# Layer 0's scores: bias and mask added per head on VectorE in the eviction, instead of in one GpSimd addition, with a newly searched order

## The chip, the cores and the metric

The kernel runs on one core of a Trainium2 chip. A core has TensorE (PE, matrix products, results into PSUM), VectorE (DVE), ScalarE (ACT), GpSimd (POOL) and SyncE (SP, which here issues all DMAs). Each engine works through its own queue in order; semaphores order the engines among each other. The metric is the device time of one execution in microseconds (us). The kernel before takes 2370.53 us, the median of three runs (2370.43 to 2375.34).

## The reference, cut to what matters

Two decoder layers work on 64 sequences of 64 tokens with 256 features. Layer 0 is self attention (16 query heads, 4 key/value heads of 128, layer norm and rotary embedding on queries and keys), cross attention with a context, and a feed-forward part with a routed low-rank term; layer 1 is again self attention, cross attention and a feed-forward part. The change concerns the scores of layer 0's self attention:

```python
q = _layernorm(q, qn_g, qn_b)
k = _layernorm(k, kn_g, kn_b)
q = q * cos + _rotate_half(q) * sin
k = k * cos + _rotate_half(k) * sin
...
scores = jnp.einsum('bhqd,bhkd->bhqk', q, k) / jnp.sqrt(jnp.float32(D))
causal = jnp.triu(jnp.ones((s, s), dtype=bool), k=1)
scores = jnp.where(causal, -jnp.inf, scores)
weights = jax.nn.softmax(scores, axis=-1)
attn = jnp.einsum('bhqk,bhkd->bhqd', weights, v)
```

## The kernel before, in words

The 4096 tokens are worked in 16 groups of 256 tokens (four sequences). Phase "a" takes every group through layer 0 (`l0_attn`, `l0_xattn`, `l0_ffn`), phase "b" through layer 1 (`l1_attn`, `l1_xattn`, `l1_ffn`); between the two the group's activations are parked in DRAM. Weight preparation ("setup") runs beside the first groups.

`l0_attn` (L841) works a group in two blocks `blk` of eight query heads and two key heads, 32 blocks in all. In a block, keys, values and four pairs of query heads are projected (`proj2`, `proj_tok`, the three products of split fp16 numbers at L430 to L432) and rotated (`rope_bank`: ACT L832 and L833, DVE L834, POOL L835 and L837). The layer norm of the queries is not applied to the queries: its scale `rs` (a reciprocal root, the DVE chain L606 to L614 that ends in `nr_y`) is applied to the scores, and the query's bias gives a term of its own. So a row of scores is

    s1 = rs * (rotated q . k) + (rotated bias of q . k) + mask

The steps of it, in program order:

- DVE L908 and POOL L911 make the final keys `kf`.
- PE L919 multiplies the rotated bias with the keys into `bias_ps`, DVE L922 adds the causal mask and makes `bm`: 128 partitions (two sequences of 64 queries) x 4 x 64, one row of 64 for each half `j` of the group and each of the two key heads. Four query heads share one row.
- For each half `j`, PE L933 multiplies queries and keys for eight heads into `s_ps`, one bank of PSUM, 128 x 8 x 64, and DVE L935 takes it out with one `tensor_tensor` that multiplies by `rs`, into half of `s1` (128 x 16 x 64, fp32, in SBUF).
- POOL L937 adds `bm` to the whole of `s1` in one instruction of 1024 columns. POOL does not touch PSUM anywhere in this kernel.
- `e.gate` (L939 before, see L1004 and L1009) is the last of these instructions; the DMAs that load the next context tiles of `l0_xattn` are made to follow it.
- `softmax_rows` (L618): DVE L625 row maximum, POOL L626 subtraction, ACT L628 exponential, the sum (DVE L643, or POOL L640 and DVE L641), DVE L644 and POOL L645 the reciprocal, POOL L652 the scaling, ACT L654 and POOL L655 the split into two fp16 halves `phl`. Then a transposing DMA (L578) makes `pt` and PE L689 multiplies it with the values (`pv_block`), and `o_proj` (L709) adds the result to the residual `xt`.

In the same phase the cross attention's row maxima run on DVE (L1040, 512 instructions), its exponentials on ACT (L1074), its products on PE (L1033, L1067, L1083).

The order of all work is fixed before the kernel is built. Every step is declared with `s.o` (engine, cost in ns, what it reads and writes, the function that issues it) or `s.alt` (a choice of engines); `Sched.plan` (L255) is a list scheduler that walks through a planned time, at each step takes among the steps that can start first the one with the smallest due time, and emits the instructions in the order of their planned starts. The due times come from `PACE`, `SHIFT`, and two tables of offsets, `LEAD` (by tile name) and `FINE` (by step); `EPS`, `PEN`, `HOLD`, `SPACE`, `WINDOW` are further settings of the scheduler. `HOLD` is added to the due time of a PE step that would change the tiling of the array; `SWITCH` is what the plan charges for such a change. The tables were found by a search. Tiles come from pools by class: `B` is the eight banks of PSUM, `k4` holds `s1`, `k2` 67 tiles of 2 KiB a partition.

Of the kernel before, what the change touches and what calls it, by code (L numbers as in the profile page):

```python
# [20 lines left out]
S = 64  # L21
# [15 lines left out]
HOLD = 965  # L37
# [372 lines left out]
def c_dve(n, ap=0):  # L410
    return 72 + 1.042 * n + 63 * ap
# [429 lines left out]
def l0_attn(e, xt):  # L841
# [5 lines left out]
    for blk in range(2):  # L847
# [77 lines left out]
        for j in range(2):  # L925
            sps = s.T("B", [128, 8, S], name="s_ps")

            def f(*r, j=j):
                q, k, p = r[:4], r[4], r[5]
                for h in range(8):  # L930
                    for b in range(2):
                        t = slice(128 * j + 64 * b, 128 * j + 64 * b + 64)
                        nc.tensor.matmul(p[64 * b:64 * b + 64, h, :], q[h // 2][:, h % 2, t], k[:, h // 4, t], start=True, stop=True)  # L933
            s.o("PE", 1080, qu + [kf], [sps, s1.sub(j)], f, duty=0.65, tile=3)
            s.o("DVE", c_dve(512), [sps, rs], [s1.sub(j)], lambda p, r, t, j=j: nc.vector.tensor_tensor(  # L935
                t[:, 8 * j:8 * j + 8, :], p, bc(r[:, j, 0:2, :].rearrange("p a b -> p (a b)"), 2, S), ALU.mult))
        s.o("POOL", 2303, [bm], [s1], lambda b, t: nc.gpsimd.tensor_tensor(  # L937
            t.rearrange("p (a h) s -> p a h s", h=4), t.rearrange("p (a h) s -> p a h s", h=4), bc(b, 2, 4), ALU.add))
# [906 lines left out]
def ctx_scale(e, I, nt):  # L1845
# [15 lines left out]
EPS = 41.35  # L1861
PEN = 247.38
NQ = 1
LEAD = {
    ".xt": -7500, "a0.acc": 6500, "a0.bias_ps": -16000, "a0.bm": -112500, "a0.k_ps": -6000, "a0.kf": -4000,
    "a0.ku": -27000, "a0.ln_mv": 86500, "a0.ln_nb": -120000, "a0.ln_rs": 43000, "a0.ln_st": 60500, "a0.nr_v": -2500,
    "a0.nr_y": -92000, "a0.ohl": -35000, "a0.phl": -9500, "a0.po": -500, "a0.pt": 36500, "a0.qu": -2500,
    "a0.rb": 21500, "a0.rk": 2000, "a0.s1": -4500, "a0.s_ps": -27500, "a0.sm_mx": 120000, "a0.sm_sm": -2500,
    "a0.sq": -2000, "a0.ss": 15500, "a0.ss_t": -7000, "a0.sss": 30500, "a0.sw": 38000, "a0.v_ps": -50000,
    "a0.vt": 84000, "a0.vx": 111500, "a0.xT": -26500, "a0.xh": 112500, "a0.xhl": -29000, "a0.xt": -3000,  # L1870
    "a1.ctx1": -38500, "a1.k1": -120000, "a1.k1_ps": -24500, "a1.ksh": 26000, "a1.kst": -32000, "a1.ln_mv": 96000,
    "a1.ln_nb": -55000, "a1.ln_rs": 68500, "a1.ln_st": 120000, "a1.o1_ps": 47500, "a1.oT1": 23000, "a1.pT": -31000,
    "a1.phl": -101000, "a1.q1": 119500, "a1.q1_d": -9500, "a1.q1_ps": -56500, "a1.q1hl": 26500, "a1.q1st": 120000,
    "a1.s1": 120000, "a1.s1_ps": -90500, "a1.sm_f": -3000, "a1.sm_mx": -76000, "a1.sm_sm": 104000, "a1.v1": 90000,
    "a1.vbd": 10500, "a1.xT": 37000, "a1.xh": -8500, "a1.xhl": -6000, "a1.xt": 73500, "f0.-": -112500,
    "f0.f0_ps": -19500, "f0.f0o_ps": -14500, "f0.hT": -69000, "f0.hm": -120000, "f0.hm_ps": 20500, "f0.ln_mv": -4000,
    "f0.ln_nb": 39000, "f0.ln_rs": 42000, "f0.ln_st": 52000, "f0.xT": 78000, "f0.xh": 24000, "f0.xhl": -18000,
    "f0.xt": -11000, "f1.f1ah": 114500, "f1.f1am": -13000, "f1.f1ix": -115500, "f1.f1o": -116500, "f1.f1o_ps": -4500,
    "f1.f1s2": 73500, "f1.f1sx": 81500, "f1.gu": 8500, "f1.gu_ps": -112500, "f1.hq": -53500, "f1.hqT": 93500,
    "f1.ln_mv": 81500, "f1.ln_nb": -116500, "f1.ln_rs": -3000, "f1.ln_st": 31000, "f1.sig": 32000, "f1.xh": -10500,  # L1880
    "f1.xq": -119500, "f1.xqT": 111000, "f1.xt": 30500, "setup.-": 15500, "setup.a1am": 100500, "setup.am_ps": -4000,
    "setup.bo_ps": 70500, "setup.bo_w": -46500, "setup.cen": -72500, "setup.ctx_a": 64000, "setup.ctxa1": 99000,
    "setup.f_t": -94500, "setup.f_w": 23000, "setup.fam": -23500, "setup.fw_ps": 40000, "setup.g_G": -68500,
    "setup.g_ps": -75500, "setup.g_w": -21000, "setup.l0cols": 87500, "setup.l0ek": 7500, "setup.l0eq": -32500,
    "setup.l0w0": -3500, "setup.l0w1": -120000, "setup.l0w2": 67000, "setup.l0w3": 14000, "setup.l0w4": 96000,
    "setup.n_am1": 11500, "setup.n_o": -60000, "setup.n_ps": -116500, "setup.n_v": 120000, "setup.n_w": -28500,
    "setup.nf": 31500, "setup.p2_ar": -85500, "setup.p2_p2": -64500, "setup.rope_t": -34000, "setup.rp_tmp": -49000,
    "setup.sqj": -80000, "setup.w_a1": -25000, "setup.w_a1o": -110500, "setup.w_am1": -59000, "setup.w_f0": -77500,
    "setup.w_hl": -18500, "setup.w_l0kv": 7000, "setup.w_l0o0": -4000, "setup.w_l0o1": -7500, "setup.w_l0q0": -77000,
    "setup.w_l0q1": 26000, "setup.w_n": 47000, "setup.w_x1ki0": -30500, "setup.w_x1ki1": -15500,  # L1890
    "setup.w_x1q0": -64500, "setup.w_x1q1": 14500, "setup.x1wki0": 18500, "setup.x1wki1": 116500,
    "setup.x1wn0": 33500, "setup.x1wn1": 41000, "setup.x1wn2": 77500, "setup.x1wn3": 56000, "setup.x1wq0": 25500,
    "setup.x1wq1": -93500, "setup.xtwo": -62500, "x0.-": -120000, "x0.cT": -11500, "x0.ctx": 9000, "x0.hl": -82000,
    "x0.hl_d": -42500, "x0.ln_mv": -10000, "x0.ln_nb": -71000, "x0.ln_rs": -118000, "x0.ln_st": -103000,
    "x0.mneg": -99500, "x0.mx_ps": -37500, "x0.so": -80000, "x0.xh": 24500, "x0.xmx": -105500, "x0.xo_ps": 3500,
    "x0.xot_ps": 49500, "x0.xpt": 13500, "x0.xrc": -17500, "x0.xs_ps": -16500, "x0.xt": -41000, "x0.xt_ps": 2500,
    "x0.y": -35000, "x0.yo": -82500, "x1.acc": -38000, "x1.cTs": -120000, "x1.chl": 68500, "x1.ctx": -50000,
    "x1.gac": 42000, "x1.gjk": -34000, "x1.gy_ps": 48000, "x1.k8": -29500, "x1.ln_mv": 74500, "x1.ln_nb": -119500,
    "x1.ln_rs": -55000, "x1.ln_st": 87000, "x1.ms": -111500, "x1.phl": 6000, "x1.pt": 64000, "x1.q8": -90000,
    "x1.qk_ps": 17500, "x1.rkL": 103000, "x1.rkb": -88500, "x1.rkb_ps": -49000, "x1.rms": 24500, "x1.s1": 120000,  # L1900
    "x1.s_ps": -120000, "x1.sm_mx": -22000, "x1.sm_sm": -68500, "x1.vn": 117000, "x1.vn_ps": 68000,
    "x1.x1esc": -45000, "x1.xT": 88000, "x1.xh": 116000, "x1.xhl": 117000, "x1.xt": 23500,
}
RESV = 1e+15
TMIN = {"setup.w_a1": 1457, "setup.w_l0kv": -4579, "setup.w_x1q1": 1916, "setup.x1wki1": -18878, "setup.x1wn0": 1785, "setup.x1wn2": -1297, "setup.x1wn3": -2931, "setup.x1wq1": -2255}
FINE = dict(a=[
    (0, 1, -19000), (1, 1, -500), (2, 1, -9000), (3, 1, -13000), (4, 1, 42000), (5, 1, 22500), (6, 1, -11000),
    (7, 1, 10000), (8, 1, 15500), (9, 1, -39000), (10, 1, 1500), (11, 1, -9500), (12, 1, -12500), (13, 1, -15500),
    (14, 1, -5000), (15, 1, 13000), (16, 1, 4000), (17, 1, 9000), (18, 1, -30500), (19, 1, 21500), (20, 1, -45000),
    (21, 3, 500), (24, 1, -34000), (25, 1, 14000), (26, 1, 30500), (27, 1, 5000), (28, 1, 5500), (29, 1, -9000),  # L1910
    (30, 1, 12500), (31, 1, 7500), (32, 1, 21500), (33, 1, 23500), (34, 1, -2000), (35, 1, 44500), (36, 1, -5000),
    (37, 1, 9000), (38, 1, 10500), (39, 1, 6500), (40, 1, 24000), (41, 1, 10000), (42, 1, 6500), (43, 1, 49000),
    (44, 1, -7000), (45, 1, 9500), (46, 1, 10000), (47, 1, 3000), (48, 1, 15500), (49, 1, 10000), (50, 1, 17000),
    (51, 1, -9500), (52, 1, 9000), (53, 1, 10000), (54, 1, 10500), (55, 1, 35500), (56, 1, 3500), (57, 1, 21000),
    (58, 1, 2500), (59, 1, 4000), (60, 1, -500), (61, 1, 1500), (62, 1, -44500), (63, 1, 2000), (64, 1, 21500),
    (65, 1, -37000), (66, 1, -49500), (67, 1, -14000), (68, 1, -5500), (69, 1, -7500), (70, 1, 1000),
    (71, 1, -12500), (72, 1, 38000), (73, 1, -1000), (74, 1, 500), (75, 1, -5000), (76, 1, 4500), (77, 1, 1000),
    (78, 1, 9000), (79, 1, 2500), (80, 1, -4500), (81, 1, 5000), (82, 1, -17000), (83, 1, -12500), (84, 1, 41500),
# [100 lines left out]
FOLD = [False, True]  # L2019
SPACE = (7285, 2674)  # L2020
BURST = 1
SHIFT = -31810.49
START = (0, 3e3, 15e3, 22e3, 40e3, 3e3, 30e3, 36e3, 60e3, 70e3)
PACE = dict(a=(81129.88, 2.24), b=(66158.31, 2.05))
STEP = (15e3, 60e3, 3e3, 5e3)
# [162 lines left out]
```

## Time and profile before

| what | value |
|---|---|
| median of three runs | 2370.53 us |
| the profiled execution | 2375.9 us, its span from first to last instruction 2374.1 us |
| phase a: last `xt` of `o_proj` (L709) starts at | 1223 us |
| bias and mask on POOL (L937) | 32 instructions, 75.8 us |
| evictions of layer 0's scores on DVE (L935) | 64 instructions, 43.1 us |
| bias plus mask, `bm`, on DVE (L922) | 32 instructions, 13.1 us |

How to read the views: the busy time of an engine in a stretch is the time in which at least one of its instructions ran; matmuls overlap, so PE's rows count the length of one, and the spacing is shorter. "PEld" is the loading of weights into PE. "A <- B: t, n, m" says that engine and line A stood idle for t us in n waits, the longest m us, and that an instruction of B ended the wait. The granted clock is the share of full speed that PE got.

### The profile page before, as it was taken

What the parts mean: (1) busy time and instruction counts of PE and PEld (TensorE: products, weight loads), DVE (VectorE), ACT (ScalarE), POOL (GpSimd) and SP (SyncE); (2) the same over time, 40 slices, a digit from 0 to 9 for tenths busy, and PEclk for the clock granted to TensorE, in tenths of its full rate; (3) what the DMA queues carried; (4) which work ended last, traced back from release to release, by engine and by line L of the source; (5) the groups of instructions that cost most, each with busy time, mean ns of one, the idle gap of its engine ahead of it and who ended that gap; (6) DMA issues with size and microseconds to landing.
All of it is one profiled execution on the core that took longest, in us unless ns stands there. A gap on an engine that the chain in (4) does not pass through costs nothing. (4 is left out here: it accounts for less than half of the span.)

```text
span 2374.1 us, 69674 instructions
## 1 busy us (share of the span) xinstructions
PE 2168.2 (91%) x28232; PEld 1692.0 (71%) x28232; DVE 1828.7 (77%) x4256; ACT 1594.2 (67%) x3047; POOL 1691.1 (71%) x1793
## 2 busy tenths in 40 slices
PE   6887889988898978999988999999999999999996
PEld 5765556655565645666645788898888988889885
DVE  7577689877878778788887766778877777777766
ACT  7864878777677768788767675666566655656552
POOL 6897898776857677688945664677777667667642
PEclk9997999999899999999989999999999999999997
DMA  7744444342344234244353353444434444343322
GB/s 233 231 118 104 113 110 115 99 110 64 99 112 95 60 62 90 47 114 104 75 157 77 73 108 66 78 86 77 77 79 78 74 81 83 77 79 77 64 33 41
DMA packets 484322, 220.82 MB, mean 93 GB/s; under 512 B 340568, under 2 KB 463384, under 8 KB 484000
## 3 DMA queue, kind: packets, MB, share of 16 engines
q1 hardware_dynamic: 484000, 216.37, 40.1%
q8 instruction: 222, 3.64, 0.6%
q14 instruction: 100, 0.82, 0.1%
HBM read 89.06 MB, written 34.64 MB: 52 GB/s over the span
## 5 line engine op out<-in xcount | busy, mean ns | idle before, releaser
L1541 PE MATMUL vn_ps<-x1wn,cTs 128*64 128x256 f16 x6144 | 357.9, 273 | 0.5 <-ACT q L1282 0.5
L1074 ACT ACTIVATE xpt<-xt_ps,xes 128x512 f32<-128x512 f32 x512 | 316.2, 699 | 61.8 <-PE xt_ps L1067 56.1
L1541 PEld LDWEIGHTS <-cTs 128*64 128x64 f16 x6144 | 327.1, 110 | 17.0 <-issue 15.1
L1040 DVE TENSOR_REDUCE xmx<-xs_ps 128x2 f32<-128x512 f32 x512 | 316.5, 679 | 27.5 <-PE xs_ps L1033 27.0
L626 POOL TENSOR_TENSOR s<-s,sm_mx 128x1024 f32<-128x1024 f32 x96 | 183.6, 1913 | 196.1 <-DVE sm_mx L625 118.3
L1546 ACT ACTIVATE vn<-vn_ps 128x512 f16<-128x512 f32 x256 | 149.2, 593 | 137.8 <-PE vn_ps L1541 136.2
L1548 DVE SCALAR_TENSOR_TENSOR vn<-vn_ps,vn 128x512 f16<-128x512 f32 x256 | 170.7, 680 | 87.2 <-ACT vn L1546 86.7
L655 POOL TENSOR_TENSOR phl<-s,phl 128x512 f16<-128x512 f32 x192 | 221.9, 1166 | 17.7 <-ACT phl L654 13.4
L652 POOL TENSOR_TENSOR s<-s,sm_sm 128x512 f32<-128x512 f32 x192 | 201.5, 1062 | 7.2
L835 POOL TENSOR_TENSOR sw<-sw,rp0s 128x512 f32<-128x512 f32 x128 | 164.8, 1296 | 15.1 <-ACT sq L833 12.9
L654 ACT CAST phl<-s 128x512 f16<-128x512 f32 x192 | 118.4, 620 | 81.5 <-POOL s L652 80.9
L832 ACT COPY sw<-q_ps 64x512 f32<-64x512 f32 x256 | 146.9, 579 | 32.0 <-PE q_ps L432 24.4
L837 POOL TENSOR_TENSOR qu<-qu,sw 128x512 f32<-128x512 f32 x128 | 163.4, 1283 | 2.0
L1650 ACT ACTIVATE k<-qk_ps,x1kb 128x256 f32<-128x256 f32 x240 | 100.6, 471 | 95.1 <-PE qk_ps L432 94.8
L1083 PE MATMUL xo_ps<-xpt,xve 128*32 128x256 f32 x2048 | 150.6, 404 | 7.9 <-ACT xpt L1074 6.1
L569 ACT ACTIVATE xh<-xt,ln_nb,ln_rs 128x256 f32<-128x256 f32 x192 | 107.2, 599 | 61.2 <-POOL ln_nb L566 60.8
L430 PE MATMUL q_ps<-xT,l0w 128*128 128x256 f16 x512 | 140.8, 275 | 2.0 <-ACT mneg L1044 0.8
L430 PE MATMUL acc<-l0w,ohl 128*128 128x256 f16 x512 | 141.2, 276 | 0.5 <-DVE ohl L696 0.4
L432 PE MATMUL q_ps<-xT,l0w 128*128 128x256 f16 x512 | 140.4, 274 | 0.7 <-DVE l0w L541 0.7
L431 PE MATMUL acc<-l0w,ohl 128*128 128x256 f16 x512 | 141.0, 275 | 0.0
L432 PE MATMUL acc<-l0w,ohl 128*128 128x256 f16 x512 | 140.9, 275 | 0.1
L430 PE MATMUL qk_ps<-cTs,x1wki 128*128 128x256 f16 x512 | 140.8, 275 | 0.0
(416 smaller groups left out, 6697.8 us busy)
## 6 DMA issues: line engine op xcount, KB each, us to landing
ovl<-hl_d SPq DMA_DIRECT2D x96, 128.0 KB
vx<-vt SPq DMA_DIRECT2D x64, 128.0 KB
ctx<-in_ctx_dram SPq DMA_DIRECT2D x32, 256.0 KB
hl_d<-hl SPq DMA_DIRECT2D x64, 128.0 KB
wd<-w_hl SPq DMA_DIRECT2D x32, 256.0 KB
q1st<-q_d SPq DMA_DIRECT2D x128, 64.0 KB
xt<-in_x_dram SPq DMA_DIRECT2D x16, 256.0 KB
ctx_a<-in_ctx_dram SPq DMA_DIRECT2D x8, 512.0 KB
```

The costliest lines, as they stand in the source:

```text
L430: nc.tensor.matmul(out, lh, rh, start=(st and i == 0), stop=False, **kw)
L432: nc.tensor.matmul(out, ll, rh, start=False, stop=(i == n - 1), **kw)
L626: s.o("POOL", 1900, [mx], [s1], lambda m, t: nc.gpsimd.tensor_tensor(t, t, bc(m, 2, 64), ALU.subtract))
L652: s.o("POOL", 1030, [sm], [s1.sub(j)], lambda m, t, h=h: nc.gpsimd.tensor_tensor(t[:, h], t[:, h], bc(m[:, h], 2, 64), ALU.mult))
L655: s.alt([("POOL", c_pool(482), lambda t, _, p, h=h: nc.gpsimd.tensor_tensor(pl(p, 1), t[:, h], pl(p, 0), ALU.subtract)), ("DVE", c_dves(51 ...
L835: s.o("POOL", 1225, [sg], [sw], lambda t, w: nc.gpsimd.tensor_tensor(v(w), v(w), bc(t, 1, 8), ALU.mult))
L837: ("POOL", 1225, lambda w, d: nc.gpsimd.tensor_tensor(view(d), view(d), w, ALU.add))], [sw], [dt])
L1040: nc.vector.tensor_reduce(m[:, h, bs % 4, :], p, AX.X, ALU.max))
L1074: nc.scalar.activation(t, p, AF.Exp, scale=a))
L1083: nc.tensor.matmul(o[32 * hh:32 * hh + 32, hs, :], v[:, n, a:a + 32], r[hh][:, n, :], start=(n == 0 and hs == 0), stop=(n == 1), skip_grou ...
L1541: nc.tensor.matmul(r[-1][64 * h:64 * h + 64, p, :], x[:, b // 2, a, k, t], w.part(r, c, 2 * (2 * p + h) + k), start=(n == 0), stop=(n == 5))
L1548: nc.vector.scalar_tensor_tensor(v(l), p, 2.0 ** -15, v(h), ALU.mult, ALU.subtract))
```

## The change

The 64 evictions and the 32 additions become 512 instructions on DVE, one per head and half. Each reads 64 columns of the scores from PSUM, multiplies them by the head's `rs` (one number per partition) and adds the row of `bm`. The plan charges 8 x 175 ns for a half. The eviction of a half now reads `bm`, and `e.gate` becomes the last eviction.

```diff
-HOLD = 965
+HOLD = 0
...
-            s.o("DVE", c_dve(512), [sps, rs], [s1.sub(j)], lambda p, r, t, j=j: nc.vector.tensor_tensor(
-                t[:, 8 * j:8 * j + 8, :], p, bc(r[:, j, 0:2, :].rearrange("p a b -> p (a b)"), 2, S), ALU.mult))
-        s.o("POOL", 2303, [bm], [s1], lambda b, t: nc.gpsimd.tensor_tensor(
-            t.rearrange("p (a h) s -> p a h s", h=4), t.rearrange("p (a h) s -> p a h s", h=4), bc(b, 2, 4), ALU.add))
+
+            def f(p, r, b, t, j=j):
+                for h in range(8):
+                    nc.vector.scalar_tensor_tensor(t[:, 8 * j + h, :], p[:, h, :], r[:, j, h // 4, h % 4:h % 4 + 1],
+                                                   b[:, 2 * j + h // 4, :], ALU.mult, ALU.add)
+            s.o("DVE", 8 * 175, [sps, rs, bm], [s1.sub(j)], f)
         e.gate = s.ops[-1]
...
-EPS = 41.35
-PEN = 247.38
+EPS = 41.45
+PEN = 318
...
-SPACE = (7285, 2674)
+SPACE = (7280, 2674)
...
-SHIFT = -31810.49
+SHIFT = 13751.24
...
-PACE = dict(a=(81129.88, 2.24), b=(66158.31, 2.05))
+PACE = dict(a=(81129.88, 2.24), b=(65853.97, 2.01))
...
-WINDOW = (5, 6)
+WINDOW = (5, 5)
```

The tables `LEAD`, `FINE` and `TMIN` are replaced as a whole, so nearly every instruction of the kernel changes its place in its queue, also in layer 1. The steps themselves are otherwise the same. Some steps with a choice of engines fall differently: of the evictions of layer 1's queries and keys, 22 were on DVE (L1646) and 5 are; the others move to ACT (L1650).

## Prediction

> **What bounds the kernel now.** I read the page's busy shares and its slices first, then the busy time by stage, then what TensorE (PE) waits for in the stage that the change touches, then the rows of the instructions that go and of the nearest relatives of those that come.
>
> The page's first part and the clock row of its slices (busy time, share of the span, instructions; each digit a tenth):
>
> ```profile
> PE 2168.2 (91%) x28232; PEld 1692.0 (71%) x28232; DVE 1828.7 (77%) x4256; ACT 1594.2 (67%) x3047; POOL 1691.1 (71%) x1793
> ...
> PEclk9997999999899999999989999999999999999997
> ```
>
> The busy time by stage (length, then PE, PEld, DVE, ACT, POOL, granted clock, DMA share, GB/s):
>
> ```profile
> 0.00:225.00 225.00, 175.56 (x1579) 136.35 (x1580) 156.19 (x404) 148.53 (x298) 179.34 (x182) 0.92 0.62 180
> 225.00:1225.00 1000.00, 888.99 (x10262) 602.72 (x10261) 805.96 (x1882) 749.71 (x1357) 772.84 (x750) 0.95 0.38 95
> 1225.00:1345.00 120.00, 106.52 (x1334) 69.78 (x1329) 94.36 (x229) 86.87 (x171) 68.08 (x85) 0.91 0.40 81
> 1345.00:2290.00 945.00, 935.26 (x14175) 830.07 (x14176) 718.90 (x1629) 582.24 (x1174) 643.67 (x745) 1.00 0.40 77
> ```
>
> The reader is to see two different kernels. From 1345 to 2290 us (layer 1) PE is busy 99% at full clock: only matmuls taken out would shorten it, and none are. From 225 to 1225 us (layer 0, where the change is) PE has 111 us without work, and a granted clock of 0.95 costs up to 5% of 889, some 44 us more. So in this stage 155 us are lost, and each microsecond of idle PE has come with 0.4 us of lost clock (44 / 111). I price a microsecond of PE waiting at 1.4. No engine is full: VectorE (DVE) 81%, GpSimd (POOL) 77%.
>
> Who keeps PE waiting in that stage (total, times, longest):
>
> ```profile
> PE po L689 <- DMA pt<-phl: 8.2, 11, 1.3
> PE f_ps L430 <- DMA xT<-xhl: 6.4, 4, 2.4
> ...
> PE xt_ps L1067 <- DVE nr_y L614: 5.0, 4, 2.2
> PE s_ps L933 <- POOL kf L911: 4.7, 5, 2.2
> ...
> PE v_ps L430 <- DMA xT<-xhl: 2.9, 4, 1.6
> ```
>
> The transposed loads named here are fed by POOL (phl at L655, xhl at L590), so POOL stands behind 8.2 + 6.4 + 4.7 + 2.9 = 22.2 us. The lines that name DVE add up to 40.6 us, 8.9 of them for weight preparation, which leaves 31.7. Neither is alone the bound.
>
> **The change part by part.** The rows concerned: what goes, then the relatives of what comes (minimum/median/maximum ns).
>
> ```profile
> L935 DVE TENSOR_TENSOR s<-s_ps,nr_y x64: 628/682/694, 89.8 to 1173.1; 128x512 f32<-128x512 f32 x64
> L937 POOL TENSOR_TENSOR s<-s,bm x32: 2347/2361/2725, 93.1 to 1177.2; 128x1024 f32<-128x1024 f32 x32
> L1104 DVE TENSOR_TENSOR y<-xot_ps,xrc x128: 161/214/225, 242.1 to 1408.3; 128x64 f32<-128x64 f32 x128
> L1154 DVE SCALAR_TENSOR_TENSOR f_ps<-f_ps,m,f0rank x32: 155/226/234, 313.5 to 1430.6; 128x8 f32<-128x8 f32 x32
> L1168 DVE SCALAR_TENSOR_TENSOR xt<-f0o_ps,f0u,xt x32: 467/474/485, 317.3 to 1437.7; 128x256 f32<-128x256 f32 x32
> ```
>
> Removed from POOL: 32 adds of 2.36 us, 75.6 us. Removed from DVE: 64 evictions. They stand 0.59 us apart when one follows another (two in 1.27 us, each 0.68), so 38 us. Added to DVE: 512 `scalar_tensor_tensor` of 128x64 out of PSUM with a per-partition factor, which the trace does not show in this size. From below: L1104, 64 columns without such a factor, takes 0.36 us for two, so 0.145 apart, 1.16 us for eight. From above: L1168 takes 0.474 for 256 columns and L709 0.746 for 512 (1.06 ns a column), so 64 columns take 0.27 alone; eight with no overlap take 2.16. Nearest is L1154, the same operation out of PSUM with such a factor: two in 0.38 us are 0.15 apart, and 56 more columns add 0.06. I take 0.20, so 1.6 us for eight: +1.0 us per half, **+64 us on DVE** (+36 to +100). In the middle stage lie 27 of the 32 blocks (five of the adds start before 225 us): POOL falls from 773 to 709 of 1000, DVE rises from 806 to 860 (836 to 890).
>
> A rule that speaks against the change: the Trainium skill, "VectorE: DVE Perf Modes", section "The TRN2 errata", advises tiles of 512 elements or more, because every instruction pays its fixed cost again. Its figure for PSUM sources, 120 + columns cycles at 0.96 GHz, makes an estimate of 1.53 us for eight against 0.66 for one, +56 us in all, where the rows make +64; by it the DVE term of the sum would be a little smaller and nothing else would change.
>
> What becomes of the chain: in the order of the instructions on PE, old and new, the bias product stands behind both score batches (32 of 32 blocks in the new order, 31 in the old). Formerly the evictions did not need it, and 51 of the 64 stood ahead of the `bm` addition on DVE. Now they must follow it. From the end of the bias product to the row maximum that was 0.41 (`bm`) + 2.36 (POOL); it becomes 0.41 + 2 x 1.6. The chain is not shorter by its work (0.8 us longer); what it loses is the crossing to POOL and the place in POOL's queue, where L937 held the queue 17.3 us for `bm` and 10.4 for the eviction. DVE waits at one place for PE (the bias product) instead of two; the row maxima of the cross attention (L1040) stand behind it. In the new order `bm` and the two evictions stand within 2 to 6 places of each other in nearly every block, so the wait is paid once. The wait for the scores today is 27.3 us for all blocks. A score bank of PSUM stays taken some 3 us longer (bias, `bm`, eight instead of one); there are eight banks, I cost it at nothing, and without that cover it is a PE wait of up to 3 us per block.
>
> PE pays or gains as follows.
> (1) POOL is less late. Of the 22.2 us half goes, 11 x 1.4 = **-15** (0 to -31). Waiting that goes as load/(1 - load) would fall from 3.40 to 2.44, 28%, directly, and the same relief reaches ScalarE, which waits 16.9 us for L652 and 16.2 us for L566 in this stage.
> (2) DVE is later. 31.7 us grow at least with the load, 860/806, +2; at most with load/(1 - load), 4.15 to 6.14, +48%, +15. I take +4, x 1.4 = **+6** (+3 to +21; at 890 of 1000 +42), near the low end because DVE idles in the stage mostly for PE and ScalarE.
> (3) The first 225 us: POOL is 80% busy and DVE 69%; five adds, 11.8 us, leave the fuller engine: **-5** (0 to -12).
> (4) The new order. Counted along PE's queue, changes between the tilings of the array fall from 1167 to 1149; such a change shows as 0.21 us ahead of L1033 in the timeline: **-4** (0 to -4). DVE gives 17 query and key evictions of 0.69 us (L1646) to ScalarE (L1650), in the stage where PE is 99% busy: nothing. The matmuls from a block's last score to its first product with the values are of the same amount in both orders. The loads of the next group's context, which wait for the block's last score instruction, now follow DVE instead of POOL; SyncE has no wait of note there: nothing.
> Sum: -15 + 6 - 5 - 4 = **-18 us**. The profiled execution took 2375.9 us (span 2374.1 and 1.8 around it), which makes 2358; it lies 5.4 above the median of the three runs, 2370.5, so on the scale of the median I predict **2352 us**.
>
> **Rivals.**
> *DVE becomes the late engine (slower).* Place: layer 0, DVE's queue between `bm` and the row maxima. Price: if its waits grow as load/(1 - load) and the eight take the upper bound, (2) becomes +42 and the sum +18: 2388. It decides from about 1.7 us for eight: there (2) is 24, all that the others bring. For it: DVE is already the fuller engine there, and the work given to it per block (2.0 us) nearly equals what POOL gives up (2.36). Against: in the stretch from 300 to 400 us DVE is 90% busy with PE no worse than elsewhere.
> *The relief is hidden (no change).* POOL idles 23% of the stage anyway, and the chain is no shorter; (1) and (3) near zero, (2) and (4) cancel: 2370. That the instruction does not do what it says belongs here: the scores are now evicted later than before, since the bias product stands behind them.
> *The new order is worth more by itself.* From 1025 to 1185 us PE is 94% busy (149.7 of 160) at clock 1.00. If half of the 155 us lost in the middle stage went, as there, the gain would be some 50 to 75 us less DVE's share: 2320. For it: nearly every instruction of layer 0 changes its place. Against: POOL itself keeps PE waiting for only 4.7 us.
>
> **How the numbers follow.** My forecast 0.38; the better order 0.14; no change 0.12; DVE late 0.36. A measurement tells apart some 0.2%, 5 us. That makes faster 0.52, same 0.12, slower 0.36. The range runs from the better order, 2322, to a little past the slower rival, 2394, which leaves out about 2 in 10; the forecast's own part is 2330 to 2365.
>
> **What would show it.** The eight evictions: 0.20 us apart (0.145 to 0.27). DVE busy in all +64 less some 17 us of moved evictions; POOL -76. Middle stage: PE's waits for transposed loads below 22 us, for DVE some 36 and not above 47, its clock at 0.96 or more; the stage from 1345 us unchanged at 99%. I am wrong if layer 0 ends later than now although POOL waits less (DVE late), or if PE's lines on DVE and on loads both stay as they are.

## The result and the profile after

The changed kernel takes **2434.41 us** (median of four runs, 2430.63 to 2438.17), the kernel before beside it 2372.94 (2370.43 to 2377.25): 1.0259 times as long, with a 95% interval of 1.0241 to 1.0278, or 61 us more. The profiled execution has a span of 2434.3 us. (Lines from L939 on in the code before are two higher in the code after.)

The first part of the page and the clock row of its slices, after (columns as shown for the kernel before):

```profile
PE 2179.6 (90%) x28232; PEld 1706.1 (70%) x28232; DVE 1889.8 (78%) x4679; ACT 1613.8 (66%) x3089; POOL 1618.1 (66%) x1761
...
PEclk9997999999999889999989999999999999999998
```

DVE is 61 us busier than before (forecast 64 less some 17 for evictions that moved away; 17 is their count, at 0.69 us each they are 11.7 us, and 12.3 us come on top in layer 1, see e14), POOL 73 us less (forecast 76): the work has moved. The time has not followed. The busy time by stage, after:

```profile
0.00:225.00 225.00, 173.98 (x1559) 138.77 (x1560) 160.97 (x456) 152.69 (x305) 170.10 (x179) 0.89 0.64 179
225.00:1225.00 1000.00, 865.50 (x9799) 581.97 (x9797) 813.14 (x2167) 714.32 (x1292) 678.63 (x693) 0.94 0.36 87
1225.00:1345.00 120.00, 99.23 (x1140) 57.37 (x1140) 94.55 (x233) 88.69 (x165) 60.15 (x71) 0.90 0.44 109
1345.00:2290.00 945.00, 919.40 (x13960) 820.72 (x13953) 724.74 (x1612) 600.63 (x1223) 657.60 (x754) 1.00 0.42 80
```

From 225 to 1225 us PE does 9799 matmuls where it did 10262, with 134.5 us idle instead of 111 and a clock of 0.94 instead of 0.95. ScalarE and POOL also do less than before in the same 1000 us (714 for 750, 679 for 773): the whole stage runs slower, and no engine is full. From 1345 us on PE is busy 97.3% of the time, where it was 99.0%. (The stretches are fixed in time; the later kernel has less of the same work in them.)

The waits of PE from 225 to 1225 us sum to 131.3 us (107.5 before). Those that name DVE grew from 45.7 to 62.7, ScalarE from 37.0 to 41.9, the transposed loads from 20.1 to 21.2, POOL from 4.7 to 5.5. Some of the largest (line waited for, total, times, longest):

```profile
PE v_ps L430 <- DMA xT<-xhl: 13.1, 4, 8.2
PE ss L881 <- ACT sq L833: 8.9, 5, 3.4
PE mx_ps L1044 <- DVE xmx L1042: 7.3, 9, 2.8
...
PE f_ps L430 <- DMA xT<-xhl: 4.6, 4, 1.5
```

The same waits were 2.9 (v_ps), 0.8 (ss), 2.1 (mx_ps) and 6.4 (f_ps) before. The reader is to see that no one wait carries the loss: some are longer, single ones much longer (8.2 us), at places that have nothing to do with the scores.

The new instruction itself, its group and one block of it in time order on DVE (start, length, instruction; in brackets the idle time before it):

```profile
L938 DVE SCALAR_TENSOR_TENSOR s<-s_ps,nr_y,bm x512: 192/275/285, 96.4 to 1237.4; 128x64 f32<-128x64 f32 x171
```

```profile
1017.48 0.42 DVE L922 TENSOR_TENSOR bm<-bias_ps,mask 128x256 f32<-128x256 f32 x1 [1.69 <-PE bias_ps L919]
1017.94 1.63 DVE L938 SCALAR_TENSOR_TENSOR s<-s_ps,nr_y,bm 128x64 f32<-128x64 f32 x8
```

Eight take 1.63 us, against 0.68 for the one of 512 columns. What they wait for, PE's rows of the same block show:

```profile
1008.91 1.15 PE L933 MATMUL s_ps<-kf,qu 128*64 128x64 f32 x32
...
1014.36 1.15 PE L933 MATMUL s_ps<-kf,qu 128*64 128x64 f32 x32
...
1016.77 0.66 PE L919 MATMUL bias_ps<-kf,rp0b 128*64 128x128 f32 x8
```

The scores are in PSUM at 1010.1 and 1015.5 us and stay there until the bias product, last of the three, ends at 1017.4; DVE stands 1.69 us for it.

Where along the kernel the time is lost, by the start of the last residual addition of a group: that of the feed-forward part in layer 0 (L1168 in the code before) and that of the cross attention in layer 1 (L1568), in us:

| milestone | before | after | difference |
|---|---|---|---|
| layer 0, group 4 | 556 | 571 | +15 |
| layer 0, group 8 | 876 | 921 | +45 |
| layer 0, group 12 | 1154 | 1198 | +44 |
| layer 0, group 16 | 1438 | 1466 | +28 |
| layer 1, group 2 | 1485 | 1538 | +53 |
| layer 1, group 16 | 2343 | 2403 | +60 |

Layer 0's first eight groups cost 45 us; groups 9 to 16 seem to win back 17, and from there to layer 1's group 2 another 25 appear; layer 1 adds 7. The two phases overlap here and the new settings start phase b later (see e14), so the 17 and the 25 may in part be the same work in another order; this is not shown.

### The profile page after: what moved, and what is told of

Read it like the earlier page. It is cut to its first block, busy times and chain, and to the rows that moved or that the text cites. A ratio compares the mean times of both kernels' runs of the same rounds, so it can differ in the third digit from the quotient of the medians.

```text
span 2434.3 us, 70325 instructions
## 1 busy us (share of the span) xinstructions
PE 2179.6 (90%) x28232; PEld 1706.1 (70%) x28232; DVE 1889.8 (78%) x4679; ACT 1613.8 (66%) x3089; POOL 1618.1 (66%) x1761
## 4 chain that ended last, share of the span: by engine, by line
PE 40%; POOL 20%; DVE 16%; ACT 10%; DMA 7%; issue 5%; SPq 1%; POOLq 0%; DVEq 0%; ACTq 0%
PE vn_ps L1543 8%; DVE xmx L1042 4%; ACT xpt L1076 4%; PE qk_ps L430 3%; POOL phl L655 3%; PE qk_ps L432 3%; PE qk_ps L431 3%; POOL s L652 3%; PE xo_ps L1085 2%; DMA pT<-phl 2%; PE s_ps L1664 2%; DVE s L938 2%; POOL sw L835 2%; POOL s L626 2%; PE acc L1566 1%
## 5 line engine op out<-in xcount | busy, mean ns | idle before, releaser
L655 POOL TENSOR_TENSOR phl<-s,phl 128x512 f16<-128x512 f32 x192 | 223.8, 1177 | 32.6 <-ACT phl L654 31.4
L1652 ACT ACTIVATE k<-qk_ps,x1kb 128x256 f32<-128x256 f32 x252 | 105.6, 472 | 74.7 <-PE qk_ps L432 72.9
L430 PE MATMUL q_ps<-xT,l0w 128*128 128x256 f16 x512 | 143.0, 279 | 2.4 <-DVE s L938 1.0
L432 PE MATMUL q_ps<-xT,l0w 128*128 128x256 f16 x512 | 142.8, 279 | 0.8 <-DVE l0w L541 0.8
L431 PE MATMUL q_ps<-xT,l0w 128*128 128x256 f16 x512 | 142.9, 279 | 0.0
```

The source lines that it names most:

```text
L430: nc.tensor.matmul(out, lh, rh, start=(st and i == 0), stop=False, **kw)
L431: nc.tensor.matmul(out, lh, rl, start=False, stop=False, **kw)
L432: nc.tensor.matmul(out, ll, rh, start=False, stop=(i == n - 1), **kw)
L655: s.alt([("POOL", c_pool(482), lambda t, _, p, h=h: nc.gpsimd.tensor_tensor(pl(p, 1), t[:, h], pl(p, 0), ALU.subtract)), ("DVE", c_dves(51 ...
```

## The experiments

The change has two parts that can be parted: the instructions, and the order. "Old order" below is the order of the kernel before: its tables and costs are kept, so that every instruction stands where it stood, and only what a step issues is replaced. "New order" is the same with the tables and costs of the changed kernel. Differences are read from the ratios to the kernel before on the same chip; 0.01 is 23.7 us.

**e1: eight evictions in the old order, POOL's addition kept.** The mask is added twice (in the eviction and in `bm`).

```diff
-            ... nc.vector.tensor_tensor(t[:, 8 * j:8 * j + 8, :], p, bc(r..., 2, S), ALU.mult)
+            ... [nc.vector.scalar_tensor_tensor(t[:, 8 * j + h, :], p[:, h, :],
+                 r[:, j, h // 4, h % 4:h % 4 + 1], e.mask, ALU.mult, ALU.add) for h in range(8)]
```

> The order of the kernel before, instruction for instruction, but each of the 64 score evictions is done by eight scalar_tensor_tensor of 64 columns (0.19 us apart in the trace after the change, so 1.6 instead of 0.6 us, some 60 us more on VectorE in all); they add the causal mask, which the later addition on GpSimd then adds a second time, and the GpSimd addition stays. DVE-load theory (the longer evictions themselves cost the time): +35 to +65 us over the kernel before, 2405 to 2435. Order theory (the newly searched order is what costs): +0 to +15, 2372 to 2387. Theory of the wait for bm (the eviction now waits for the bias product): also +0 to +15, since here it doesn't wait for it.

Measured: 2398.26 us, 1.0133 [1.0106, 1.0161], +31 us, between the two expectations.

**e2: the old order without POOL's addition** (bias and mask are left out).

```diff
-        s.o("POOL", 2303, [bm], [s1], lambda b, t: nc.gpsimd.tensor_tensor(...))
+        s.o("POOL", 2303, [bm], [s1], lambda b, t: None)
```

> The order of the kernel before with the 32 GpSimd additions of bias and mask left out (scores without bias and mask). It measures what GpSimd's relief of 76 us is worth by itself. My prediction's terms (1) and (3): -20 us, 2352. If the relief is hidden: 2365 to 2373. All three theories of the slowdown are silent on it; the smaller the gain, the less the change had to win.

Measured: 2361.01 us, 0.9975 [0.9959, 0.9990], -6 us. The 75 us that POOL is spared bring 6. Where the rest goes, POOL's own waits from 225 to 1225 us show: they sum to 209.9 us before and to 269.9 in e2. Before, the wait of the addition for `bm` and that of the subtraction for the row maximum:

```profile
POOL s L937 <- DVE bm L922: 17.3, 5, 11.7
POOL s L626 <- DVE sm_mx L625: 17.2, 10, 6.0
```

The second line in e2:

```profile
POOL s L626 <- DVE sm_mx L625: 49.6, 15, 16.0
```

POOL is ready sooner and stands until DVE has made the row maximum; in the changed kernel this line is 76.6 us. In the old order POOL was hardly what the chain waited for.

**e3: both, in the old order.** Eight evictions that add the mask, no addition on POOL; the bias is left out, and nothing waits for `bm`.

```diff
  (the edits of e1 and e2 together)
```

> The order of the kernel before with both halves of the change and without its new wait: eight instructions per eviction that add the mask, no GpSimd addition (the bias is left out of the scores; bm is still made, but nothing waits for it). DVE-load theory: +20 to +50, 2393 to 2423. Order theory: -20 to +5, 2352 to 2378. Theory of the wait for bm: -20 to +5 as well.

Measured: 2385.05 us, 1.0073 [1.0049, 1.0098], +17 us, again between the expectations; against e2 the eight evictions cost 0.0098, 23 us, against 31 us in e1 beside a busier POOL (the difference of the two lies within their intervals).

**e4: the new order with one eviction per half**, bias and mask left out: e2's steps in the other order. (Steps with a choice of engines fall as in the changed kernel: DVE does 4231 instructions where it did 4256, ACT 3089 for 3047.)

```diff
-                for h in range(8):
-                    nc.vector.scalar_tensor_tensor(...)
+                nc.vector.tensor_tensor(t[:, 8 * j:8 * j + 8, :], p, bc(r..., 2, S), ALU.mult)
```

> The order of the changed kernel, but each eviction is one tensor_tensor of 512 columns that multiplies by rs (bias and mask are left out; bm is made at its place in the queue). VectorE does some 60 us less than in the changed kernel, and GpSimd no addition. DVE-load theory: back to 2360 to 2390. Order theory: stays at 2410 to 2430 (40 to 60 over the kernel before). Theory of the wait for bm: 2405 to 2425, as the evictions stand behind bm in VectorE's queue here too.

Measured: 2421.71 us, 1.0228 [1.0206, 1.0250]. With the same steps, the new order takes 0.0253, 60 us, longer than the old. The middle stage of e2, then of e4:

```profile
225.00:1225.00 1000.00, 892.54 (x10358) 603.25 (x10355) 809.40 (x1904) 759.82 (x1375) 716.41 (x735) 0.96 0.39 96
```

```profile
225.00:1225.00 1000.00, 869.49 (x9935) 585.92 (x9933) 773.30 (x1805) 725.77 (x1316) 688.00 (x704) 0.95 0.36 87
```

All four engines are less busy in e4, DVE at 773 of 1000 us: the engines stand apart more often, and none is the bound. Two smaller parts can be named. Over the whole run the granted clock is 0.963 against 0.968, on PE's 2170.6 busy us an estimate of 11 us. And DVE is busy 1838.9 us against 1819.3, although it has fewer instructions: some take longer (see e14); at e16's 0.4 us per us that is an estimate of 8 us. Against e2, layer 0 is 50 us late at group 8, 30 at group 16; layer 1 is 55 us late at its group 2 and 62 at group 16. This is the changed kernel's pattern (its table above), without its instruction.

**e5: the new order with the old operations**, one eviction of 512 columns per half, and POOL's addition issued behind the block's second eviction.

```diff
+                nc.vector.tensor_tensor(t[:, 8 * j:8 * j + 8, :], p, bc(r..., 2, S), ALU.mult)
+                done.append(j)
+                if len(done) == 2:
+                    nc.gpsimd.tensor_tensor(... bc(b, 2, 4), ALU.add)
```

> The order of the changed kernel with the operations of the kernel before: one tensor_tensor per half, and one GpSimd addition of bias and mask per block, put into GpSimd's queue at the place of the block's second eviction. With the last runs (old order with short evictions and no addition 2361, new order with the same work 2422) the order theory says that the order alone costs some 55 us: 2420 to 2435 here. If the new order were good only for operations that it was searched for, and bad because of the fused ones' wait, it would be 2375 to 2400.

Measured: 2447.20 us, 1.0324 [1.0302, 1.0346]. In this order the new instruction is 15 us better than the old pair (1.0259 against 1.0324): POOL's additions cost 23 us here (e5 against e4), the eight evictions 7 (after against e4, the intervals overlap). The same edit has opposite signs in the two orders. The addition is put into POOL's queue by hand here, not by the plan, which might have found a better place for it.

**e8: e4 with each eviction moved up** to right behind its own batch of scores on PE.

```diff
-        order.sort(key=lambda o: (o.start, o.grp, o.idx))
+        order.sort(key=lambda o: (self.early[o].end + 197 if o in self.early else o.start, o.grp, o.idx))
```

> As e4_new_order_one (new order, one tensor_tensor per half, bias and mask left out), but in VectorE's queue each eviction is moved from behind bm to the planned end of its own score batch on TensorE; all other instructions keep their order. Theory of the wait for bm: most of the 55 us comes back, 2370 to 2390. Order theory: 2410 to 2425, within some 10 us of the 2422 of e4_new_order_one.

Measured: 2423.21 us, 1.0220 [1.0195, 1.0244], the same as e4. From the first matmul of a batch to the end of its eviction a score bank is now held 2.25 us on average, in e4 5.96 (2.73 before, 7.50 after). So the late evictions and the banks they hold are not what makes the new order slow.

**e9: the whole change in the old order**, each eviction moved behind its block's `bm` wherever it stood ahead of it.

```diff
-        order.sort(key=lambda o: (o.start, o.grp, o.idx))
+        order.sort(key=lambda o: (max(o.start, self.late[o].start + 1) if o in self.late else o.start, o.grp, o.idx))
```

> The whole change in the order of the kernel before: eight fused instructions per half that read bm, no GpSimd addition, and each eviction that stood ahead of bm in VectorE's queue is moved behind it; all else keeps its place. Order theory: e3_old_order_both (2385, +18) plus at most 10 for the wait: 2380 to 2398, some 40 us faster than the changed kernel. Theory of the wait for bm: 2410 to 2435, near the changed kernel.

Measured: 2440.59 us, 1.0303 [1.0274, 1.0332], +71 us, where the theory that the new order is the whole loss gave 2380 to 2398, and that of the wait for `bm` 2410 to 2435. The first falls in this form, and the wait costs a little more than the second gave: in the old order, where 51 of 64 evictions stood ahead of `bm`, the wait for the bias row costs 0.023, 55 us, more than e3. A bank of scores is held 7.87 us (e3: 3.94), and from the first score of a block to its row maximum it is 14.53 us (12.49). 2.0 us in each of 32 blocks are 65 us, if all of it lies on the path. What the instruction needs is late in an order that was not made for it, and the search had reason to look for another.

**e10: the changed operations planned with the tables of the kernel before**, without a new search.

```diff
  (open tables and settings of the kernel before: LEAD, FINE, TMIN, HOLD, EPS, PEN, SPACE, SHIFT, PACE, WINDOW)
```

> The changed operations planned with all the settings and tables of the kernel before (the entries of the two steps that are gone dropped), without a new search. If the tables fit one set of operations only, layer 0 falls apart: over 2480. If tables carry over and the new ones are just worse: 2380 to 2400.

Measured: 2557.9 us in one run. It says little of the instruction: `FINE` gives its offsets by a step's position in its group, and a group has two steps fewer, so most offsets fall on another step. It shows what the order can be worth: 123 us between two plans for the same steps.

**e11: the whole change in the old order, with the bias product first.** The product stands ahead of both batches of scores on PE, `bm` ahead of the first eviction on DVE, and the evictions keep their places. Nothing is left out.

```diff
+        for mb, mk, mm, ev in self.blocks:
+            key[mb] = min(mb.start, min(o.start for o in mm) - 1)
+            key[mk] = min(mk.start, min(o.start for o in ev) - 1)
-        order.sort(key=lambda o: (o.start, o.grp, o.idx))
+        order.sort(key=lambda o: (key[o], o.grp, o.idx))
```

> The whole change (eight instructions per half that read the row of bias plus mask, no addition on GpSimd) in the order of the kernel before, but with the bias product put ahead of both score batches on TensorE, and bm ahead of the first eviction on VectorE, so that the evictions keep their old places. Theory A (what costs some 55 us in e9 beyond e3 is that the evictions must wait for a late bias product): about e3's time, ratio 1.004 to 1.012. Theory B (the additional operand costs whatever its place, or the early bias product holds up TensorE as much as the late one held up VectorE): ratio 1.02 or more.

Measured: 2398.52 us, 1.0123 [1.0084, 1.0162]. Theory A comes nearest, just above the 1.012 that it gave, and theory B's 1.02 is out: 43 us of e9's 55 are gone, 12 are left over e3 (the intervals touch). A bank is held 3.88 us again. This kernel computes all that the changed one does and is 0.0136, 32 us, faster than it, with an order that took two moves per block.

**e12: e3 with the banks held.** Behind each `bm` DVE reads one column of each of the two score banks once more, so that they come free as late as in e9, while the scores come out as early as in e3. The bias is left out.

```diff
+            for v in sp:
+                if v.real is not None:
+                    nc.vector.tensor_copy(e.touch, v.real[:, 0, 0:1])
```

> e3 (old order, eight instructions per half at their old places with the mask as third operand, no addition on GpSimd; the bias is left out) and, right behind bm, one more read of one column of each of the two score banks, 64 small VectorE instructions in all. The scores come out of PSUM as early as in e3, but the banks stay taken until bm is done, as in e9. If the banks of PSUM are what e9 ran short of (bank theory): ratio 1.02 or more, like e9. If it was the late scores (latency theory): e3 and at most 8 us for the small reads, ratio 1.005 to 1.013.

Measured: 2410.76 us, 1.0177 [1.0139, 1.0215]: between the two theories. The banks are held 7.0 us on average (e9: 7.9). 0.0104, 25 us, come on top of e3, and by the two intervals it could be 15 us or 35; the 62 small reads of 0.15 us are 10 us of DVE, 4 us at the price that e16 finds below. So some 20 of the 55 us go to the banks, and the remainder, by subtraction, to the late scores; that last step is not measured by itself.

**e15 and e16: the extra DVE time at another place.** e2, and behind each block's row maximum DVE work that nobody reads: in e15 ten small instructions, in e16 two reductions of the mask. Bias and mask are left out of the scores in both.

```diff
         nc.vector.tensor_reduce(m, t, AX.X, ALU.max)
+        e15: 10 x nc.vector.scalar_tensor_tensor(e.load, e.mask, m[:, 0:1], e.mask, ALU.mult, ALU.add)
+        e16: nc.vector.tensor_reduce(e.load[:, 0:16], bc(e.mask, 1, 16), AX.X, ALU.max)
+             nc.vector.tensor_reduce(e.load[:, 16:24], bc(e.mask, 1, 8), AX.X, ALU.max)
```

> e2 (old order, one eviction of 512 columns per half, no addition on GpSimd; bias and mask are left out) and, behind the row maximum of each block, ten small scalar_tensor_tensor of 128x64 on VectorE whose result nobody reads: about the time that the eight instructions per half add to a block (3.16 against 1.27 us), but behind the scores instead of in front of them, with no PSUM bank held. Load theory (VectorE's own load costs the 24 to 31 us of e1 and e3): e3's ratio, 1.004 to 1.011. Place theory (it costs because it stands between the scores and the softmax and holds the bank): near e2, 0.996 to 1.001.

Measured: 2546.36 us, 1.0753 [1.0724, 1.0783], outside both expectations, because the dose was wrong: the group of the ten (busy time, mean of one, idle before it) reads

```profile
L629 DVE SCALAR_TENSOR_TENSOR load<-mask,sm_mx 128x64 f32<-128x64 f32 x320 | 197.2, 616 | 11.4
```

that is 197 us instead of 61. Why is told under the hardware below. e16 repeats the question with an instruction whose duration holds still:

> e2 again (bias and mask left out), with the extra VectorE time behind each block's row maximum taken by two reductions of the mask (1024 and 512 columns, one operand from SBUF, some 1.9 us together by the row of the row maximum, 1.21 us for 1024) instead of e15's ten small instructions, which stretched from 0.285 to up to 2.0 us beside GpSimd: 61 us more of VectorE in all, as e3 has. Load theory: e3's ratio, 1.004 to 1.011. Place theory (the cost lies in the late scores and the bank held): 0.996 to 1.001.

```profile
L628 DVE TENSOR_REDUCE load<-mask x32: 1202/1210/1218, 99.6 to 1199.6; 128x16 f32<-128x1024 f32 x32
L629 DVE TENSOR_REDUCE load<-mask x32: 673/677/685, 100.7 to 1200.7; 128x8 f32<-128x512 f32 x32
```

Measured: 2396.40 us, 1.0083 [1.0063, 1.0103]. The busy time of the engines over the whole run, in e2, e3 and e16:

```profile
PE 2157.5 (92%) x28232; PEld 1687.2 (72%) x28232; DVE 1819.3 (77%) x4256; ACT 1593.8 (68%) x3047; POOL 1615.0 (68%) x1761
PE 2166.2 (91%) x28232; PEld 1690.4 (71%) x28232; DVE 1880.0 (79%) x4704; ACT 1594.1 (67%) x3047; POOL 1617.0 (68%) x1761
PE 2176.3 (91%) x28232; PEld 1697.2 (71%) x28232; DVE 1879.8 (78%) x4320; ACT 1597.7 (67%) x3047; POOL 1616.7 (68%) x1761
```

Against e2, e16 takes 26 us more and e3 23. The added reductions do not stand in front of POOL's subtraction: it starts 0.08 us behind the row maximum in most blocks of e2 and of e16 alike. So it is VectorE's load that costs, at both places in the block: about **0.4 us of time for 1 us of VectorE** in layer 0 of the old order (26 / 60.5). The place theory is refuted for the eight evictions themselves.

**e14: layer 1's new tables alone.** Layer 0 with the operations and tables of the kernel before; offsets, pace and shift of phase b and the window from the changed kernel.

```diff
-SHIFT = -31810.49
-PACE = dict(a=(81129.88, 2.24), b=(66158.31, 2.05))
-WINDOW = (5, 6)
+SHIFT = 13751.24
+PACE = dict(a=(81129.88, 2.24), b=(65853.97, 2.01))
+WINDOW = (5, 5)
```

> Layer 0 with the operations and the tables of the kernel before, layer 1 with the new tables (offsets, pace and shift of phase b). If the 7 us by which layer 1 of the changed kernel is longer belong to its new order: ratio 1.002 to 1.005, with PE's busy share from 1500 us on near 97 to 98%. If they are an echo of the late layer 0: 0.999 to 1.001.

Measured: 2399.78 us, 1.0136 [1.0103, 1.0169]: more than expected. From its group 2 to group 16 layer 1 takes 874 us (before 858, after 865). What PE waits for from 1500 us on, in e14 and then in the changed kernel:

```profile
PE ctx L1327 <- DMA pT<-phl: 17.9, 11, 2.6
PE gu_ps L1784 <- DMA xqT<-xq: 8.7, 11, 0.8
```

```profile
PE ctx L1329 <- DMA pT<-phl: 10.2, 11, 1.0
PE gu_ps L1786 <- DMA xqT<-xq: 8.8, 11, 0.9
```

Two transposed loads, one wait in most groups each: in the kernel before the first is not in this list and the second is 2.3 us. The second load carries `xq`, which DVE makes with two instructions per group. Before, then in the changed kernel:

```profile
L1770 DVE TENSOR_SCALAR xq<-xh x32: 273/286/315, 1430.2 to 2350.4; 128x256 bf16<-128x256 f32 x32
L1772 DVE TENSOR_SCALAR xq<-xh x32: 274/290/1253, 1485.8 to 2410.0; 128x256 bf16<-128x256 f32 x32
```

In the changed kernel 13 of the 32 take 1.13 to 1.25 us, and each of these ends 0.15 us behind the end of a POOL instruction, `phl` (L655) in 12 of them. The 11 waits of `gu_ps` stand in exactly the 11 groups in which the second of the two is stretched; e4 has 13 such instructions and e14 12; the kernel before, e2, e3, e9, e11 and e16, with layer 1 in its old order, have none above 0.32 us. So the 8.8 us of PE's waits for `xqT` come from DVE instructions that now stand beside POOL. Layer 1's loss belongs to its own new order and is no echo of layer 0. How much of the changed kernel's 7 us each setting brings is not told apart, since a plan with other neighbours is another plan. The shift, which moves phase b's due times 45.6 us later, goes with layer 0 ending 30 us earlier here (1408 for 1438) and layer 1's group 2 not earlier at all (1491 for 1485).

## Why the prediction was wrong, point by point

The forecast was 2352 us (-18); measured is +61. Two ways lead from the old kernel to the new one: the operations first, in the old order, and the order last; or the order first, with the old operations (e5).

| step | forecast | measured, old order | measured, new order |
|---|---|---|---|
| POOL's 75 us go: (1) and (3) | -15 -5 | -6 (e2) | -23 (e4 against e5) |
| 61 to 64 us more on DVE: (2) | +6 | +23 (e3 against e2) | +7 (after against e4) |
| eviction behind the bias row | 0 | +12, placed early (e11 against e3) | in the order |
| new order: (4) | -4 | +32 (after against e11) | +77 (e5) |
| sum | -18 | +61 | +61 |

- **The step that failed: "(4) The new order ... -4 (0 to -4)".** I priced the order by the one thing I could count, changes of the array's tiling (1167 to 1149; by the array sizes that the traces print they are 1105 and 1044), and gave it no loss at all in the range. The same steps take 60 us longer in it (e4 against e2). The changes of tiling are fewer, so they are not the cause, nor are the late evictions and their banks (e8). The trace shows longer waits at many lines and four engines that are less busy. The plan that the kernel itself computes agrees in sign: with the new tables and costs it ends 49 us later than with the old (2375.5 against 2326.5 us by the plan's own clock). So the order is not a better one even by the plan; why the search kept it is not on record. In layer 1 part of the loss is traced to `xq` beside POOL (e14). Which of the offsets makes it slow in groups 1 to 8 of layer 0, where most of the loss is, stays open.
- **"I cost it at nothing" (the score bank held some 3 us longer, and the wait for the bias row).** Held are 7.50 us for 2.73, not 3 us more but 4.8. Bought at the best place tried the dependency costs 12 us (e11, the intervals of e11 and e3 touch), at its worst 55 (e9), of which some 20 for the banks (e12). I had the right sentence, "51 of the 64 stood ahead of the `bm` addition. Now they must follow it", and drew no price from it. My count that the chain is no shorter was right: from a block's first score to its row maximum it is 13.49 us after, 12.10 before.
- **(2) DVE is later, +6.** The amount of work was right (1.63 us for eight, forecast 1.6; the estimate from the Trainium skill, "VectorE: DVE Perf Modes", section "The TRN2 errata", was 1.53), the price of it was not: 0.4 us per us of DVE in the old order, where I took 0.1 (6 us for 64), near the low end. The 31.7 us of waits that I started from left out smaller lines; all lines without weight preparation give 35.3. That is the slower rival's mechanism, DVE as the late engine. I set its threshold at 1.7 us for eight; e3 is slower than before at 1.63. In the new order the same instructions cost only 7 us, as far as the busy times tell because DVE stands idle more there (773 of 1000 us in e4, 809 in e2).
- **(1) and (3), POOL's relief, -20.** In the old order 6, in the new one 23. "Half of the 22.2 us goes" was a choice without a row behind it (my own load formula gave 28%, 9 us at 1.4); what the trace did show, and I passed over, is that POOL itself already waited 17.2 us for the row maximum behind the addition and 17.3 for `bm` in front of it. In the old order the relief became a longer wait for the row maximum (49.6 us in e2). The no-change rival was right about this part.
- **Layer 1, "nothing".** 7 us, from the new order (e14): PE's two waits there are for the transposed loads of `phl` and of `xq`, the latter behind DVE instructions that GpSimd holds up. As far as the waits tell it is not from the 17 evictions that went to ScalarE.
- Of the signs that I named: "layer 0 ends later although POOL waits less" came half true. Layer 0 ends 28 us later, and PE's waits for DVE, without weight preparation, are 52 us (62.7 less 10.4), past the 47 that I set; but POOL's waits in the stage grew from 210 to 309 us. PE's waits for transposed loads, to be below 22, are 21.2, which says nothing, as they were 20.1 before. The clock, which was to be 0.96 or more, is 0.94, and the stage from 1345 us, which was to stay at 99%, is at 97.3%.

No kernel here beats the one before with all of its computation. The sum in the old order leaves little room: the relief of POOL is worth 6 us there, so by these prices a way of adding bias and mask on DVE may cost 15 us of DVE in all (an estimate, 6 / 0.4), half a microsecond per block. Whether a third order would do better with the new instruction is not tested.

## What to carry to other kernels

Here the order was worth more than the instruction it was searched for: before believing a gain from one operation, run the new operation in the old order and the old operation in the new order, because a change of tables cost 60 us with the same work here. Moving work from one engine to a fuller one has two prices, what the fuller engine's time costs and what the other's relief brings: 0.4 and 0.1 us per us in the old order, but 0.1 and 0.3 in the new one. Neither follows from the busy shares: ask first which of the two engines the chain is waiting for. And a new operand is a new due date: when an instruction comes to read what used to be needed later, move its producer up first (e11 against e9: 43 us from two moves).

## What the runs showed of the hardware that was not expected

Ten `scalar_tensor_tensor` of 128x64 with both tensors in SBUF (e15) took 0.285 us each when POOL was idle, and up to 2.03 us beside it. One block's ten on DVE, and POOL in the same time (start, length, instruction):

```profile
124.73 6.99 DVE L629 SCALAR_TENSOR_TENSOR load<-mask,sm_mx 128x64 f32<-128x64 f32 x10
```

```profile
124.78 1.91 POOL L631 TENSOR_TENSOR s<-s,sm_mx 128x1024 f32<-128x1024 f32 x1 [0.38 <-DVE sm_mx L626]
126.64 0.63 POOL L1019 TENSOR_SCALAR xve<-cT 128x512 f32<-128x512 f32 x1
127.23 1.27 POOL L842 TENSOR_TENSOR qu<-qu,sw 128x512 f32<-128x512 f32 x1
128.45 1.27 POOL L840 TENSOR_TENSOR sw<-sw,rp0s 128x512 f32<-128x512 f32 x1
```

The first four of the ten end at 126.76, 127.34, 128.58 and 129.80 us, each some 0.07 us behind the end of a POOL instruction (126.69, 127.27, 128.50, 129.72): each waits for the POOL instruction that is running. In the whole run 98 of the 320 take more than 0.4 us, and every one of the 98 ends 0.07 to 0.09 us behind the end of a POOL instruction. The Trainium skill, "GPSIMD Engine Reference", section "Key points", says that GpSimd shares its SBUF interfaces with VectorE and contends with DVE instructions that have two SBUF inputs; this trace agrees, and shows the size. The changed kernel's evictions, with one tensor from PSUM and one from SBUF, show none of it: 192 to 285 ns for all 512. The larger reductions of e16, with one input from SBUF, hold 1.202 to 1.218 us as well. One input is no safeguard by itself, though: the `xq` instructions of layer 1 (e14) read one SBUF tensor and go from 0.29 to 1.25 us beside POOL.
